# First expert layer: results weighed in the expert's own loop, the router's weights sent along in the slots, and the gather turned into transfers that add

## The chip, the cores and the metric

The kernel runs on one core of one Trainium2 chip. The metric is the device time of one launch in microseconds (us): the median of three runs. A profiled execution gives the trace: every instruction of the engines TensorE (PE), VectorE (DVE), ScalarE (ACT), GpSimd (POOL), of the queue of SyncE (SP), and every DMA, with times counted from the start of the span.

## What is computed

Four layers on x of 4 sequences of 512 tokens of width 256: a cross attention with 8 heads over a context of 1601 rows, a mixture of experts (E = 8, two experts for each token, a fixed capacity), a second cross attention, and a second mixture of experts. The change is in the first mixture of experts. Cut to what matters, the reference does this:

```python
x = x + attention(ctx, layernorm(x))
xf = layernorm(x).reshape(-1, 256)                       # 2048 tokens
scores = softmax(xf @ w_router)                          # 8 columns
expert_weights, top_experts = top_k(scores, 2)
# every (token, choice) gets a place in its expert's list, first come first served;
# beyond capacity = 512 places it is dropped
xb = zeros(8 * 512, 256).at[slot].set(xf[src])
y  = gelu(xb @ w1[e]) @ w2[e]                            # per expert
out[src] += expert_weights * y[slot]                     # dropped choices add 0
x = x + out + bias
# then the second attention and the second mixture of experts
```

## The kernel before

The kernel is one program that is fully laid out in advance. It has four stages, seen in the trace by the lines that run in them.

Stage A, 0 to about 1550 us: the first attention. Batch after batch, `route(b)` is slipped in between: it normalizes x[b] into `xn` (L159), computes the router's scores `sc`, takes the two best (values to `prob`, slot numbers to `slot`), and `send` (L316) scatters the token rows into `slot_x`, a tensor in device memory with 4096 rows (SLOTS) of 256 floats. One scatter moves 128 rows; there are 4 tiles of 128 tokens (t) and 2 choices (k) for each of the 4 batches, so 32 of them. The slots are set to zero early on by 8 transfers (`clear_slots`, L193) from a zeroed piece `empty` of the tile `scrap`.

Stage B, about 1550 to 1916 us: the experts. Each expert's list is worked through in two halves of 256 slots (`all_experts(0, ...)`, then `all_experts(1, ...)`). For each: `fetched` loads `sx` from `slot_x` (L1247) and the two weight matrices, `turned` transposes, `hidden` does the first product and the gelu on ACT (L1276), `results` does the second product, copies it out of PSUM (L1291), and stores it to `slot_y` (L1292). Between the halves there is a branch that repeats the experts if the halves were not filled as hoped; it is a meeting point for all engines. Right behind it stands `collect(0)`: for t, for k, POOL sets a buffer `g` to zero (L334) and gathers 128 rows of `slot_y` into it (L335). `add_collected(0)` (L352) multiplies each gathered tile by its `prob` column and adds it to x[0]. Then `queries(0)` starts the second attention's work on x[0]: moments of each tile (L127, L128), `ve` (L137), the square root `rs` on ACT (L144), the scaling (L159). `all_experts(1)` runs at the same time.

Stage C, about 1916 to 2560 us: the second attention, in 16 units of 13 steps. The order of the instructions on PE, DVE, ACT and POOL is written out by hand here: a table `at` holds what is to be issued in which step (`put`). For batch b, `collect(b + 1)` puts one gather in each of the steps max(52b - 28, 0) + 1 onwards (8 steps), `add_collected(b + 1)` puts two adds each in the steps 52b + 10, 12, 14 and 16, and `queries(b + 1)` begins at 52b + 12. From step 4 on, one step after the other, `clear_rows` sets 41 pieces of `rows_a` and `rows_b` (the second expert layer's lists) to zero by transfers on SP (L395) out of the small tile `empty`. Every second of these is preceded by a POOL memset that writes a marker into `empty` again (L1647); so the POOL memset waits for the two transfers that still read `empty`, and the next two transfers wait for the memset. `load_queries(u)` (L1160) brings the queries of unit u into `asked` on the same SP queue, at step 13u - 12. The maxima `tops` (L1195) and the running sums (L1471) are DVE's main work.

Stage D, about 2560 us to the end: the second mixture of experts. Its results are added onto the output in device memory by indirect transfers with an add (`add_out`, L1788).

Outside the stretches whose order is written out, the order of the instructions of each engine is chosen at compile time by a planner, from its own idea of durations. `keep_in_program_order` pins some transfers.

## Time and profile before

| | |
|---|---|
| median of 3 runs | 2829.24 us (2828.84 to 2831.44) |
| the profiled execution's own time | 2828.22 us |
| its span in the trace | 2826.2 us |
| PE busy | 2706.3 us of the span |
| DVE busy | 1468.9 us |
| ACT busy | 940.0 us |
| POOL busy | 260.0 us |
| PE busy in 1750 to 1930 us | 169.27 of 180 us |
| L335, gather without an add | 32 times, 1003 ns of POOL each (median) |
| L334, memset of `g` | 32 times, 314 ns of POOL each |
| L352, weigh and add | 32 times, 484 ns of DVE each |
| L1788, scatter with an add | 38 times, 1594 ns of POOL each |

Busy time is the sum of an engine's instructions. A line of the waits says which engine stood before which line, and what released it. A line of the timeline has the start, the duration, engine and line, and in brackets how long the engine had been idle before it and what ended that. Transfers issued by POOL are on the DMA queue q0, those of SP on q1.

### The profile page before, as it was taken

How to read it: one execution, taken by the hardware profiler on the slowest of the kernel's cores; microseconds unless marked ns; L12 is line 12 of the kernel's file. 1: busy time of each engine (PE TensorE's matmuls, PEld its weight loads, DVE VectorE, ACT ScalarE, POOL GpSimd, SP SyncE). 2: the span in 40 equal slices, each digit the busy share in tenths (PEclk: the TensorE clock that was granted, in tenths of full speed). 3: DMA queues.
4: the chain of work that ended last, by engine and by line, in shares of the span. 5: the costliest groups of instructions: out<-in, count | busy, mean ns of one | idle time of the engine just before them, and what ended most of it. 6: DMA issues, size and time to landing. Idle time of an engine off the chain costs nothing. (4 is left out here: it accounts for less than half of the span.)

```text
span 2826.2 us, 36019 instructions
## 1 busy us (share of the span) xinstructions
PE 2706.3 (96%) x13566; PEld 1851.0 (65%) x13566; DVE 1468.9 (52%) x2343; ACT 940.0 (33%) x1362; POOL 260.0 (9%) x292
## 2 busy tenths in 40 slices
PE   5999999999999999999999899998999898889998
PEld 2666666666766666766666687774455454458887
DVE  6544547544476444545444421137887878872111
ACT  3333334323233332333233211214444444442221
POOL 0000000100000000001000002001110201022542
PEclk9999999999999999999999999999999999999999
DMA  5444443433343344334334545535631111025573
GB/s 164 110 115 113 104 103 95 114 95 84 95 119 91 102 100 100 89 85 113 95 84 125 176 154 175 169 97 144 178 81 40 38 31 54 33 71 193 166 229 89
DMA packets 196435, 311.95 MB, mean 110 GB/s; under 512 B 43319, under 2 KB 117368, under 8 KB 193560
## 3 DMA queue, kind: packets, MB, share of 16 engines
q1 hardware_dynamic: 157512, 227.52, 29.4%
q0 software_dynamic: 14160, 46.31, 5.5%
q10 hardware_dynamic: 24576, 35.68, 4.9%
q8 instruction: 111, 1.82, 0.3%
q14 instruction: 76, 0.62, 0.1%
HBM read 111.73 MB, written 51.34 MB: 58 GB/s over the span
## 5 line engine op out<-in xcount | busy, mean ns | idle before, releaser
L842 DVE TENSOR_REDUCE top<-ps_s 128x1 f32<-128x2113 f32 x128 | 301.8, 2358 | 581.0 <-PE ps_s L834 581.0
L871 PE MATMUL ps_o<-pT,v 128*128 128x256 f32 x2176 | 521.6, 381 | 0.5 <-DVE inv L849 0.5
L834 PE MATMUL ps_s<-kT,qT 128*128 128x512 f32 (+1 forms) x1280 | 489.0, 526 | 5.8 <-ACT attn L848 5.8
L871 PEld LDWEIGHTS ps_o<-pT,v 128*128 128x128 f32 x2176 | 409.9, 191 | 115.1 <-issue 68.4
L848 ACT ACTIVATE attn<-ps_s,top 128x2113 f32<-128x2113 f32 x128 | 259.0, 2024 | 476.7 <-DVE top L842 452.0
L834 PEld LDWEIGHTS ps_s<-kT,qT 128*128 128x128 f32 x1280 | 241.6, 191 | 252.5 <-issue 236.6
L863 DVE STREAM_TRANSPOSE pT<-swapped 128x2176 f32<-128x2176 f32 x128 | 312.4, 2441 | 33.8 <-DMA swapped<-attn 23.7
L1195 DVE TENSOR_REDUCE tops<-ps_s 128x2 f32<-128x1024 f32 (+1 forms) x224 | 238.3, 1106 | 102.9 <-PE ps_s L1184 101.7
L783 PE MATMUL ps_k<-kvin,wkv 128*128 128x512 f32 (+1 forms) x640 | 263.6, 535 | 4.1 <-DVE mv_g L721 2.1
L1453 PE MATMUL ps_w<-asked,keyed 64*128 64x256 f32 (+1 forms) x1664 | 225.2, 405 | 35.1 <-DVE tops L1195 33.9
L817 PE MATMUL ps_v<-wkv,kvin 128*128 128x256 f32 x1088 | 254.5, 381 | 0.0
L1466 ACT ACTIVATE pT<-ps_w 128x1024 f32<-128x1024 f32 x192 | 189.8, 1022 | 150.7 <-PE ps_w L1453 139.4
L817 PEld LDWEIGHTS ps_v<-wkv,kvin 128*128 128x128 f32 x1088 | 204.8, 190 | 34.9 <-issue 4.5
L1453 PEld LDWEIGHTS ps_w<-asked,keyed 64*128 64x128 f32 (+1 forms) x1664 | 150.3, 188 | 110.2 <-DVE tops L1195 53.5
L1471 DVE TENSOR_TENSOR sum<-sum,pT 128x1024 f32<-128x1024 f32 x176 | 214.8, 1221 | 13.5 <-PE ps_o L1480 4.9
L796 ACT ACTIVATE kT<-ps_k,bqk 128x512 f32<-128x512 f32 (+1 forms) x160 | 96.9, 620 | 265.9 <-PE ps_k L783 130.5
L783 PEld LDWEIGHTS ps_k<-kvin,wkv 128*128 128x128 f32 x640 | 116.2, 192 | 78.6 <-issue 68.0
L824 ACT COPY v<-ps_v 128x512 f32<-128x512 f32 x144 | 79.9, 561 | 215.9 <-PE ps_v L817 143.9
L1184 PE MATMUL ps_s<-kv,qT 32*128 32x512 f32 (+1 forms) x1024 | 134.7, 553 | 9.3 <-DVE tops L1195 5.1
L1269 PE MATMUL ps_h<-sxT,w 128*128 128x256 f32 x512 | 116.1, 384 | 3.7 <-ACT hT L1276 3.7
L1283 PE MATMUL ps_y<-w,hT 128*128 128x256 f32 x512 | 115.1, 380 | 0.0
L1269 PEld LDWEIGHTS ps_h<-sxT,w 128*128 128x128 f32 x512 | 97.9, 192 | 20.5 <-ACT hT L1276 4.5
(302 smaller groups left out, 2525.2 us busy)
## 6 DMA issues: line engine op xcount, KB each, us to landing
swapped<-attn SPq DMA_DIRECT2D x1536, 68.0 KB, 2.0
swapped<-attn ACTq DMA_DIRECT2D x512, 68.0 KB, 2.2
w<-in_w_dram SPq DMA_DIRECT2D x32, 1024.0 KB, 6.0
rows_b<-empty SPq DMA_DIRECT2D x36, 530.0 KB, 4.4
w_e<-in_wall_dram SPq DMA_DIRECT2D x5, 2052.0 KB
cw<-in_ctxT_dram SPq DMA_DIRECT2D x4, 1601.0 KB
keyed<-kv SPq DMA_DIRECT2D x32, 200.1 KB, 3.6
ctx_b<-in_ctx_dram SPq DMA_DIRECT2D x3, 1536.0 KB
```

Of the source, the lines that this page charges most:

```text
L783: nc.tensor.matmul(ps[:, :n], lhsT=wkv[:, c, hs], rhs=kvin[:, c, : NB - 1, k, :] if k < 4 else kvin[:, c, NB - 1, :, :], start=c == 0, sto ...
L817: nc.tensor.matmul(ps[:, k, :], lhsT=flat_kvin[c][:, j * P : (j + 1) * P], rhs=wkv[:, c, cols], start=c == 0, stop=c == DC - 1,)
L834: nc.tensor.matmul(flat[:, j0 : j0 + n], lhsT=qT[:, t * P : (t + 1) * P], rhs=kT[:, j0 : j0 + n], start=True, stop=True,)
L842: nc.vector.tensor_reduce(top, flat[:, :L], AX.X, ALU.max, negate=True)
L848: nc.scalar.activation(attn[:, :L], flat[:, :L], AF.Exp, bias=top, accum_out=total)
L863: nc.vector.transpose(pT[:, :, k * P : (k + 1) * P].rearrange("p c (a i) -> p a c i", a=4), swapped.rearrange("p a (c i) -> p a c i", i=32),)
L871: nc.tensor.matmul(ps, lhsT=v[:, j - parts[part][0], (h % 2) * DH0 : (h % 2 + 1) * DH0], rhs=pT[:, j, :], start=j == 0, stop=j == NB - 1,)
L1195: nc.vector.tensor_reduce(tops[u][:, t : t + at // n, 2 * pair : 2 * pair + 2, j0 // 512], of, AX.X, ALU.max,)
L1269: nc.tensor.matmul(ps[:, f, :], lhsT=w1[:, c, (f0 + f) * P : (f0 + f + 1) * P], rhs=sxT[:, c, :], start=c == 0, stop=c == DC - 1,)
L1453: nc.tensor.matmul(ps[:r, s, pair * QH : (pair + 1) * QH], lhsT=keyed[o][64 * s : 64 * s + 64, pair, j * P : j * P + r], rhs=asked[u % 3][ ...
L1466: nc.scalar.activation(pT[:r], ps[:r], AF.Exp)
L1471: nc.vector.tensor_tensor(sums[u, 0], sums[u, 0], pT, ALU.add)
```

## The change

The rows in the slots become 264 floats wide (XROW): behind the 256 values of a token stand its 8 router scores. They are copied there before the choice is made, sent along by the same scatter and fetched with `sx`. The expert's own column of them, `share`, is copied out in `turned`, and `results` multiplies by it when it empties PSUM; an unused slot holds zeros. `slot_y` so holds weighed results. `collect` has no buffer, no memset and no add on DVE any more: the gather itself adds onto x[b], tile by tile, and its order is now k outside and t inside. `add_collected` and `prob` are gone, with their steps in the table of stage C and their place in `keys_next`.

```diff
-    slot_x = dram.tile([SLOTS, D], F32, name="slot_x")
+    slot_x = dram.tile([SLOTS, XROW], F32, name="slot_x")            # XROW = D + E
...
-                zeros.unsqueeze(1).to_broadcast([P, 4, D]),
+                zeros.unsqueeze(1).to_broadcast([P, 4, XROW]),
...
-        xn = wide_rt.tile([P, NT, D], F32, tag="xn", name="xn")
+        xw = wide_rt.tile([P, NT, XROW], F32, tag="xn", name="xw")
+        xn = xw[:, :, :D]
...
+            nc.vector.tensor_copy(xw[:, :, D:], sc)
             for k in range(2):
-                pk, ck, hk, cand = prob[k][:, mine_b], small(f"c{k}"), wide(f"hot{k}"), wide("cand")
+                pk, ck, hk, cand = small("pk"), small(f"c{k}"), wide(f"hot{k}"), wide("cand")
...
-                        in_=xn[:, t, :],
+                        in_=xw[:, t, :],
...
         def one_of(t, k):
             j = b * NT + t
-            g = gat.tile([P, D], F32, tag="g", name="g")
-            nc.gpsimd.memset(g, 0.0)
             nc.gpsimd.indirect_dma_start(
-                out=g,
+                out=x[b][:, t, :],
                 out_offset=None,
                 in_=slot_y[:, :],
                 in_offset=bass.IndirectOffsetOnAxis(ap=slot[k][:, j : j + 1], axis=0),
                 bounds_check=SLOTS - 1,
                 oob_is_err=False,
+                compute_op=ALU.add,
             )
-            got.append(g)
-
-        return got, [lambda t=t, k=k: one_of(t, k) for t in range(NT) for k in range(2)]
-
-    def add_collected(b, got, tiles=range(NT)):
-        for t in tiles:
-            for k in range(2):
-                j = b * NT + t
-                xs = x[b][:, t, :]
-                nc.vector.scalar_tensor_tensor(
-                    xs, got[2 * t + k], prob[k][:, j : j + 1], xs, ALU.mult, ALU.add
-                )
+        return [lambda t=t, k=k: one_of(t, k) for k in range(2) for t in range(NT)]
...
-        empty = scrap[:, 0, :]
+        empty = scrap.rearrange("p t d -> p (t d)")[:, :XROW]
...
-            sx = two.tile([P, CT, D], F32, tag="sx", name="sx")
+            sx = two.tile([P, CT, XROW], F32, tag="sx", name="sx")
...
+            share = two.tile([P, CT], F32, tag="share", name="share", bufs=3)
+            nc.vector.tensor_copy(share, sx[:, :, D + e])
...
-            nc.vector.tensor_copy(y, ps)
+            nc.vector.tensor_tensor(y, ps, share.unsqueeze(2).to_broadcast([P, CT, D]), ALU.mult)
             nc.sync.dma_start(slots(slot_y, e, half), y)
...
-                if k == 6:
-                    add_collected(0, got0)
...
-                for k, f in enumerate(steps):
+                for k, f in enumerate(collect(b + 1)):
                     put(max(s0 - 28, 0) + 1 + k, f)
-                for t in range(NT):
-                    put(
-                        s0 + 10 + 2 * t,
-                        lambda b=b, got=got, t=t: add_collected(b + 1, got, (t,)),
-                    )
```

`share` is handed on from `turned` through `hidden` to `results`; the tile that `output_bias` borrows from `scrap` moves from its second row to its third.

More of the change, by code (lines that the diff above doesn't have):

```diff
@@ L43 @@
 SLOTS = E * CAP
+XROW = D + E
 HALF = CAP // 2
@@ L224, in xattn_ffn_twice @@
     reached = const.tile([P, 2, E], F32, name="reached")
-    prob = [const.tile([P, NX], F32, name=f"prob{k}") for k in range(2)]
     slot = [const.tile([P, NX], I32, name=f"slot{k}") for k in range(2)]
@@ L327, in collect @@
     def collect(b):
-        got = []
         def one_of(t, k):
             j = b * NT + t
-            g = gat.tile([P, D], F32, tag="g", name="g")
-            nc.gpsimd.memset(g, 0.0)
             nc.gpsimd.indirect_dma_start(
-                out=g,
+                out=x[b][:, t, :],
                 out_offset=None,
@@ L896, in output_bias @@
         def output_bias():
-            values_bias = scrap[:, 1, :P]
+            values_bias = scrap[:, 2, :P]
             ps = ps_t.tile([P, D], F32, tag="t", name="ps_bo")
@@ L1260, in turned, with hidden @@
             nc.vector.tensor_copy(sxT, tp.rearrange("p c t q -> p c (t q)"))
-            return e, half, sxT, w1, w2
-        def hidden(e, half, sxT, w1, w2):
+            share = two.tile([P, CT], F32, tag="share", name="share", bufs=3)
+            nc.vector.tensor_copy(share, sx[:, :, D + e])
+            return e, half, sxT, share, w1, w2
+        def hidden(e, half, sxT, share, w1, w2):
             hT = two.tile([P, FC, HALF], F32, tag="hT", name="hT")
@@ L1276, in hidden, with results @@
                 nc.scalar.activation(hT[:, f0 : f0 + 2, :], ps, AF.Gelu_apprx_tanh)
-            return e, half, hT, w2
-        def results(e, half, hT, w2):
+            return e, half, hT, share, w2
+        def results(e, half, hT, share, w2):
             ps = ps_y.tile([P, CT, D], F32, tag="y", name="ps_y")
@@ L1358, in xattn_ffn_twice @@
                     results(*hidden(*turned(*fetched(e, half))))
-        got0, steps = collect(0)
-        for f in steps:
+        for f in collect(0):
             f()
@@ L1612, in xattn_ffn_twice @@
                 put(s0 + 1, lambda b=b: begin(b + 1))
-                got, steps = collect(b + 1)
-                for k, f in enumerate(steps):
+                for k, f in enumerate(collect(b + 1)):
                     put(max(s0 - 28, 0) + 1 + k, f)
-                for t in range(NT):
-                    put(
-                        s0 + 10 + 2 * t,
-                        lambda b=b, got=got, t=t: add_collected(b + 1, got, (t,)),
-                    )
                 def later(b=b):
```

## Prediction

> **What bounds the kernel now.** I read the page first, then the windows by stage, then what PE waits for, then the timelines around each place where the change acts.

> ```profile
> PE 2706.3 (96%) x13566; PEld 1851.0 (65%) x13566; DVE 1468.9 (52%) x2343; ACT 940.0 (33%) x1362; POOL 260.0 (9%) x292
> ...
> 1750.00:1930.00 180.00, 169.27 (x819) 129.82 (x819) 50.41 (x75) 35.56 (x56) 16.03 (x21) 0.96 0.45 144
> 1950.00:1975.00 25.00, 20.85 (x210) 10.71 (x206) 21.63 (x30) 9.92 (x12) 0.29 (x3) 0.93 0.66 179
> 2090.00:2115.00 25.00, 25.00 (x226) 14.90 (x223) 22.87 (x34) 13.31 (x18) 9.04 (x14) 1.00 0.09 25
> 2260.00:2285.00 25.00, 25.00 (x224) 15.56 (x218) 22.91 (x32) 11.87 (x15) 0.00 (x0) 1.00 0.20 48
> ```

> PE is the bound (second column of the windows: PE busy, fourth: DVE). A gain or loss is a gain or loss of PE's idle time. The last three windows hold the adds of batches 1, 2 and 3 that the change takes away: only the first has idle PE time.

> Where does PE wait near the change? In stage B, behind the branch, and in stage C, at three adds and at the start of unit 4:

> ```profile
> 1769.04 0.20 ACT L144 ACTIVATE rs<-ve 128x4 f32<-128x4 f32 x1 [3.97 <-DVE ve L137]
> 1771.20 3.78 PE L1269 MATMUL ps_h<-sxT,w 128*128 128x256 f32 x8 [3.38 <-ACT hT L1276]
> ...
> 1954.39 1.13 PE L1453 MATMUL ps_w<-asked,keyed 64*128 64x256 f32 x8 [1.38 <-DVE tops L1195]
> 1960.57 1.39 PE L1453 MATMUL ps_w<-asked,keyed 64*128 64x256 f32 x8 [2.33 <-DVE tops L1195]
> 2056.71 2.09 PE L1453 MATMUL ps_w<-asked,keyed 64*128 64x256 f32 x16 [1.18 <-DMA asked<-qT]
> ```

> The first pair: ACT sits at the square root for x[0] until the gathers of x[0] have landed and been added, the gelu behind it is late, and PE loses 3.38 us. The last line is a transfer of queries. It was late because on SP's queue it stands behind the zeroing of `rows_b`, and that runs in lockstep with POOL:

> ```profile
> SPq L395 <- POOL empty L1647: 62.5, 13, 6.1
> POOL empty L1647 <- DMA rows_b<-empty: 102.2, 16, 9.5
> ```

> (waits from 1916 to 2060 us). Memset, two transfers, memset: about 7 us a round, from 1924.07 until beyond 2056. So the start of unit 4 is set by POOL, SP and the DMA engines, not by PE or DVE, and PE is there 1.18 us early.

> **The change part by part.**

> *DVE's 32 adds go* (484 ns each, 15.5 us). Eight in stage B: DVE is busy 50 of 180 us there. Eight at 1952 to 1971: each pair takes 1.00 us and PE waits right behind three of them (1.38, 2.33, and 0.44 at 1972.48). At most 0.92 + 1.00 + 0.44 = 2.4 us come back. But all of it lies ahead of unit 4, which waits for `asked`: PE only gets there earlier and waits longer. Worth 0; if the zeroing did not bind, 2.4 + 1.18 = 3.6. Sixteen at 2096 to 2114 and 2264 to 2282: PE is busy 25.00 of 25.00, worth 0.

> *POOL's 32 memsets go* (314 ns), and the gathers become adding transfers. No gather of before adds, but `add_out` does:

> ```profile
> L335 POOL DMA_INDIRECT g<-slot_y,slot x32: 994/1003/1653, 1750.0 to 2115.8; - x32
> L1788 POOL DMA_INDIRECT out_dram<-y,to x38: 1549/1594/1621, 2559.5 to 2816.0; - x38
> ```

> (nanoseconds: least, median, most). Bounds for an issue are 1.00 and 1.59 us; I take 1.59, since it is the only row that adds. The gap between issues is 0.30 us where nothing is waited for. On the DMA engines:

> ```profile
> q0 software_dynamic: 384, 1.04, 13.6%
> rows_b<-empty SPq DMA_DIRECT2D x8, 530.0 KB, 4.7
> g<-slot_y,slot POOLq DMA_INDIRECT x8, 5.4
> ...
> q0 software_dynamic: 437, 0.32, 18.0%
> out_dram<-y,to POOLq DMA_INDIRECT x4, 3.8
> ```

> The first is the window 1998 to 2028 us (eight gathers beside the zeroing): 13.6% of 30 us for 1.04 MB, 3.9 us of all 16 engines per MB. The second is 2800 to 2816 us (adds alone): 18.0% of 16 us for 0.32 MB, 9.0 us per MB, 2.3 times as much. [...]

> *What that does to the zeroing.* In program order four gathers of batch 1 stand ahead of the first memset of `empty` (steps 1 to 4). Before: 1918.26 to 1924.07. After: 4 x 1.59 + 3 x 0.30 = 7.26 us, so 1925.5: +1.45 (with 1.00 us an issue it would be -0.9). Then twelve gathers run inside the chain: four of batch 1 and eight of batch 2. The four rounds with two gathers of batch 2 took 7.38, 7.54, 7.50 and 7.48 us; the rounds without 7.08 in the mean. [...] Bounds 0 and +3.1; the upper one is taken, as it stands on the row. Sum: `asked` of unit 4 comes 4.5 us later, and PE with it. Behind it, unit 5's queries were issued at 2071.3 for use near 2091, so nothing more is late.

> *The waits that are added.* A k = 1 gather changes the same tile as the k = 0 gather four issues earlier and must wait for its landing. The scatters into `slot_x` show such a wait: POOL stood 71.8 us in 28 of them. Transfers to separate parts of one tile do not wait (the four of `keyed` on SP went out within 3.22 us), so I expect the four tiles of x[b] to stay independent. In stage C: four issues later is 7.6 us, landings took 5.4, and behind a waiting gather stands the memset of `empty`, which waits for its transfers anyway (4.57 and 3.45 us): 0. For batch 2 the gathers are four rounds apart in pairs: 0. Batch 3's come behind the zeroing, the old wait of POOL for DVE there (25.9 us) goes, and x[3] is needed from 2264 on: 0.

> *collect(0) in stage B.* The eight gathers went out at 1750.0 to 1759.2, one every 1.3 us; the weights of the next experts filled the DMA engines (landings 7.0 us), the last landed at about 1766.8. After: issues at 1750.0, 1751.9, 1753.8, 1755.7; the next four each wait for their first half. With 7.7 us to land under load (the four adds at 2556 to 2600 us), the fourth is in at 1763.4, the eighth goes out then and lands at 1771.1: 4.3 us later. Behind it there was one add, two moments and `ve`, 2.0 us; now one moment and `ve`, 0.8. So ACT's root comes 3 us later, and PE's 3.38 us become about 6.4: **+3.0**, if the planner leaves the root in front of the gelus. Bounds: it may move the root behind them (-3.4), or in front of more, or the landings may take the 9.2 us of the slowest add (+4.5).

> *Small parts.* `y` becomes a multiplication from PSUM with 512 columns: L573 does that in 681 ns, the copy took 692: 0. `share`, 16 copies of about 0.17 us, and four copies of `sc` (L474, 128x32, 0.18 us): DVE waits for PE in both stages (581 us at L842, 99.8 at L1291): 0; without that cover 3.4 us. Rows of 1056 bytes: scatters of 1060-byte rows land in 3.2 us (`rows_b`) and 2.6 (`rows_a`) against 2.8, so -0.2 to +0.4 each, in chains that end 30 us ahead of the load of the second half. The zeroing of `slot_x` moves 3% more, hidden by the 250 us to the first scatter. [...]

> **Sum.** +4.5 (unit 4) + 3.0 (root) = +7.5 us. The sum is made on the profiled execution (span 2826.2, its own time 2828.22); the median is 1.0 above it, and I add the sum to the median: 2829.24 + 7.5 = 2836.7.

> **The rivals.**

> 1. *Both lags* (above), 2836.7. For: both waits are in the trace already, at their edge. Own range +3 to +13 (2832 to 2842).
> 2. *One lag or none.* The planner orders stage B anew, and with the adds gone it may put the root behind the gelus (-3.4), or SP's transfer of `asked` one round earlier (7 us), so that unit 4 no longer waits and the 3.6 us of stage C count. One lag alone gives +3 to +4.5; the rest -3.4 + 4.5 = +1. So 2825 to 2833.
> 3. *Faster: POOL sends gathers at 1.00 us and the zeroing gets ahead.* Price: -0.9 at the start instead of +1.45. It decides once `asked` is in place before PE is: then 3.6 in stage C and 3.4 in stage B, -7.0, 2822. Against it: the only adding row says 1.59.
> 4. *Each adding gather waits for the one before it*, or `asked` slips by a round. With landings of 5 us in place of a step of 1.9: three waits ahead of the first memset, 3 x 3.1 = 9, and about 4 us in each later round with gathers: +12 to +40, 2841 to 2870. Against it: the `keyed` row.

> **How the numbers follow.** 0.2% of this time is 5.7 us, about what a measurement can tell from no change. Chances: case 1 0.52 (0.37 slower, 0.15 within), case 2 0.25 (0.20 within, 0.03 faster, 0.02 slower), case 3 0.08 (0.07 faster, 0.01 within), case 4 0.15 (slower). Together slower 0.54, within 0.36, faster 0.10. The range 2825 to 2848 takes in case 1 and nearly all of case 2, and the near third of case 4; 0.17 lies outside.

> **What would show it.** Right: L1788-like issues of 1.5 to 1.6 us for the gathers; the first memset of `empty` about 7.3 us after the first gather of batch 1; PE's wait for `asked` at unit 4 grown from 1.18 to some 8 us, with the three waits near 1952 to 1972 smaller; a wait of 6 us for L1276 behind L144 in stage B; windows of batches 2 and 3 unchanged. Wrong: no wait for `asked`, or gathers that go out one by one at their landings.

## The result, and the profile after

The changed kernel is slower: 2842.01 us against 2828.97 us (medians of 6 runs each on one chip), ratio 1.0051 with a 95% interval of 1.0041 to 1.0061, so +13 us where +7.5 was forecast. It lies in the stated range of 2825 to 2848 us, at the upper end of what was said for the likeliest case (2832 to 2842). On two other chips the same pair gave 1.0031 (1.0021 to 1.0040) and 1.0037 (1.0021 to 1.0052). The profiled execution after took 2845.54 us, span 2843.8, at the slow end of its runs; its span is 17.6 us above that of before.

The page's line of engines, and the same stretches as before (columns: the window, its length, then PE, PEld, DVE, ACT and POOL busy, PE's granted clock, DMA share, GB/s). Stage C begins some 3 to 4 us later than before, so the last three windows are moved by 4 us:

```profile
PE 2716.0 (96%) x13566; PEld 1854.9 (65%) x13566; DVE 1457.7 (51%) x2331; ACT 939.7 (33%) x1362; POOL 271.2 (10%) x260
...
1750.00:1930.00 180.00, 165.74 (x783) 128.32 (x783) 45.15 (x72) 33.60 (x54) 19.26 (x14) 0.95 0.46 137
1954.00:1979.00 25.00, 22.61 (x238) 11.79 (x230) 22.38 (x27) 11.64 (x14) 0.39 (x4) 1.00 0.54 144
2094.00:2119.00 25.00, 25.00 (x197) 14.33 (x193) 20.44 (x25) 14.40 (x20) 0.27 (x1) 1.00 0.05 9
2264.00:2289.00 25.00, 25.00 (x204) 14.37 (x206) 20.60 (x26) 14.70 (x21) 0.00 (x0) 1.00 0.03 7
```

Stage B lost 3.5 us of PE's busy time (169.27 to 165.74). At the adds of batch 1 PE is busier, at those of batches 2 and 3 it was full and is full. DVE has 11 us less to do, POOL 11 us more, although its 32 memsets are gone.

What PE and ACT waited for in stage B, and PE in stage C. In a timeline the brackets hold the idle time before the line and what ended it:

```profile
1759.31 1.28 ACT L145 ACT_TABLE_LOAD   x1
1771.92 0.20 ACT L145 ACTIVATE rs<-ve 128x4 f32<-128x4 f32 x1 [11.33 <-DVE ve L138]
1772.15 1.28 ACT L1269 ACT_TABLE_LOAD   x1
...
1774.09 5.76 PE L1262 MATMUL ps_h<-sxT,w 128*128 128x256 f32 x16 [6.56 <-ACT hT L1269]
...
1961.02 1.14 PE L1443 MATMUL ps_w<-asked,keyed 64*128 64x256 f32 x8 [0.46 <-DVE tops L1186]
...
1966.28 1.13 PE L1443 MATMUL ps_w<-asked,keyed 64*128 64x256 f32 x8 [1.42 <-DVE tops L1186]
...
1970.85 2.00 PE L1443 MATMUL ps_w<-asked,keyed 64*128 64x256 f32 x16
...
2063.32 3.89 PE L1443 MATMUL ps_w<-asked,keyed 64*128 64x256 f32 x16 [4.58 <-DMA asked<-qT]
```

The root `rs` of x[0] stands in front of the gelus as before, ACT has loaded the root's table at 1759.31 and then waits 11.33 us for `ve`, and PE's wait behind it has grown from 3.38 to 6.56 us. In stage C the three waits at the adds fell from 1.38, 2.33 and 0.44 us to 0.46, 1.42 and nothing. In stage B the wait for `sx` at L1250 grew too, from 0.23 to 1.72 us, just ahead of the one for `hT`. The wait for `asked` at unit 4 grew from 1.18 to 4.58 us, and the 16 matmuls behind it took 3.89 us instead of 2.09.

POOL's gathers in stage B and around the start of the zeroing:

```profile
1749.48 1.63 POOL L335 DMA_INDIRECT x<-slot_y,slot  x1 [28.12 <-DVEq L1348]
...
1756.99 1.55 POOL L335 DMA_INDIRECT x<-slot_y,slot  x1 [0.30 <-issue]
1759.81 1.55 POOL L335 DMA_INDIRECT x<-slot_y,slot  x1 [1.26 <-DMA x<-slot_y,slot]
...
1763.53 1.55 POOL L335 DMA_INDIRECT x<-slot_y,slot  x1 [0.30 <-issue]
...
1921.63 1.55 POOL L335 DMA_INDIRECT x<-slot_y,slot  x1 [156.54 <-DMA slot_y<-y]
1928.22 0.65 POOL L1631 MEMSET empty<- 128x1 f32 x1
```

and the groups of waits of SP's queue and of POOL from 1916 to 2060 us (engine, line, waited for: us in total, times, longest):

```profile
SPq L386 <- POOL empty L1631: 103.4, 18, 9.8
...
POOL empty L1631 <- DMA rows_b<-empty: 92.3, 15, 10.4
...
POOL x L335 <- issue: 6.2, 15, 0.7
```

A gather now holds POOL for 1.55 us instead of 1.00. The lines at 1756.99 and 1759.81 us are the fifth and the sixth gather of x[0]. The fifth waits for nothing; the sixth waits 1.26 us for a landing, by the order that of the second, which changes the same tile. That is the only wait of a gather for another one: in stage C the list has none. SP and POOL run in lockstep as before.

The DMA engines in 2004 to 2034 us, where the eight gathers of batch 2 run beside the zeroing (queue: packets, MB, share of 16 engines; then issues with us to landing):

```profile
q0 software_dynamic: 1076, 0.98, 25.2%
...
x<-slot_y,slot POOLq DMA_INDIRECT x8, 5.7
```

25.2% of 30 us for 0.98 MB is 7.7 us of all engines per MB, against 3.9 before: in these two windows an adding gather costs twice what a plain one does, in 1076 packets instead of 384.

**Where the time went.** The same matmul of PE, looked up in both traces from the start of each span, is early or late in the trace after as follows: ahead of the branch -0.5 us, behind `collect(0)` +3.4, at 2040 us +3.2, behind unit 4's start +9.0, at 2300 us +10.4, at 2530 us +15.1, at the end +17.6. The two steps of +3.9 and +5.8 lie at the two waits of the forecast. What is behind 2100 us goes with stretches of half clock that are not at one place: the granted clock fell to 0.5 for 37.5 us of stage C in the trace before, 64.9 in this one, and 41 to 61 in single traces of the kernels below. That part does not follow the change. From 2100 to 2810 us this trace loses 5.8 us on that of before; two kernels below that gather plainly (`plain_all`, `fac_before_asked`) lose 6.6 and 6.3, and the changed kernel taken again (`after_again`) gains 2.9.

### The profile page after: what moved, and what is told of

Same layout as the page of the kernel before. It is cut to its first block, busy times and chain, and to the rows that moved or that the text cites. A ratio compares the mean times of both kernels' runs of the same rounds, so it can differ in the third digit from the quotient of the medians.

```text
span 2843.8 us, 35938 instructions
## 1 busy us (share of the span) xinstructions
PE 2716.0 (96%) x13566; PEld 1854.9 (65%) x13566; DVE 1457.7 (51%) x2331; ACT 939.7 (33%) x1362; POOL 271.2 (10%) x260
## 5 line engine op out<-in xcount | busy, mean ns | idle before, releaser
L1443 PE MATMUL ps_w<-asked,keyed 64*128 64x256 f32 (+1 forms) x1664 | 232.7, 416 | 35.2 <-DVE tops L1186 30.5
L1276 PE MATMUL ps_y<-w,hT 128*128 128x256 f32 x512 | 115.1, 380 | 0.0
```

What stands on the lines that cost most here:

```text
L1443: nc.tensor.matmul(ps[:r, s, pair * QH : (pair + 1) * QH], lhsT=keyed[o][64 * s : 64 * s + 64, pair, j * P : j * P + r], rhs=asked[u % 3][ ...
```

## The experiments

The first four kernels ran on one chip, with before at 2830.55 us (67 runs).

**Is it the adding gathers at all?** In `plain_all` all four batches are gathered as before, with a zeroed buffer and an add on DVE (without the weight, which `results` has applied); wide rows, `share` and the multiplication stay. `plain0` does so for x[0] alone.

```diff
-                out=x[b][:, t, :],
+                out=to,                      # a zeroed tile of gat
...
-                compute_op=ALU.add,
...
+            nc.vector.tensor_tensor(xs, got[t, k], xs, ALU.add)
```

> The weights still travel in the slots and the experts weigh their own results, but all four batches are gathered as before: a zeroed buffer, a plain gather, an add on DVE (now a plain add of two tiles). Theory of the two lags (the adding gathers delay the root of x[0] in stage B and the queries of unit 4 in stage C): both waits go back to those of before, so 2829 us, +-3. Rival 'wide rows' (the 264-float rows, the share copies and the multiplication out of PSUM cost the time): it stays at 2842.

> Only batch 0 is gathered plainly and added on DVE; batches 1 to 3 keep the adding gathers. Two lags: stage B gets its 3 to 4 us back (PE's wait behind the root 3.4 instead of 6.6 us), stage C keeps its lag, so about 2838. Rival 'stage C alone': no change, 2842. Rival 'stage B alone, the rest follows from it': 2829.

`plain_all`: 2830.40 us (14 runs), ratio 1.0007 (0.9998 to 1.0016). `plain0`: 2833.54 us (22 runs), 1.0012 (1.0003 to 1.0020). PE's waits from 1740 to 2600 us that stand at the two places, first of `plain_all`, then of `plain0`:

```profile
PE ps_h L1276 <- ACT hT L1283: 3.2, 1, 3.2
PE ps_w L1460 <- DMA asked<-qT: 0.6, 1, 0.6
```

```profile
PE ps_w L1460 <- DMA asked<-qT: 6.9, 1, 6.9
PE ps_h L1276 <- ACT hT L1283: 2.8, 1, 2.8
```

With plain gathers both waits are about as before (3.4 and 1.2 us), and so is the time: the rows of 1056 bytes, `share` and the multiplication cost nothing that a measurement can tell; the interval leaves room for 4.5 us. With plain gathers for x[0] alone, only the first wait goes back; the second stays long. So each wait belongs to its own gathers: the one in stage B to those of x[0], the one at unit 4 to those of batches 1 to 3. For `plain0` 2838 us were expected and 2833.54 came; the changed kernel itself did not run on this chip, so what `plain0` gained on it there is not known.

How long a wait is does not say what it costs. Unit 4 in `plain_all` and in `plain0`:

```profile
2056.23 2.10 PE L1460 MATMUL ps_w<-asked,keyed 64*128 64x256 f32 x16 [0.61 <-DMA asked<-qT]
```

```profile
2057.37 3.86 PE L1460 MATMUL ps_w<-asked,keyed 64*128 64x256 f32 x16 [6.91 <-DMA asked<-qT]
```

The wait is 6.3 us longer, but unit 4 starts only 1.1 us later: PE was there 5.2 us sooner (2050.46 instead of 2055.62), most of it the 4 us that it gains where the adds of batch 1 are gone. To the 1.1 us come some 2.5 us behind the wait, where the 16 matmuls take 3.86 us instead of 2.10, as they take 3.89 in the trace after at a granted clock of 0.50. Together that is 3.6 us; the medians of the two kernels differ by 3.1.

**Is it the two waits?** `after_root` keeps the adding gathers, but binds the root of x[0] on ACT to program order, so that it no longer stands in front of the gelus. `after_asked` issues the transfer of queries for units 4, 8 and 12 seven steps earlier; in its trace that of unit 4 went out at 2035.96 instead of 2058.71.

```diff
+        if b == 0:
+            with in_order(nc.scalar):
+                root = ln_root(turns, mv, NT, ve)
...
-            put(NM * u - 12, lambda u=u: load_queries(u))
+            put(NM * u - (19 if u % 4 == 0 else 12), lambda u=u: load_queries(u))
```

> The changed kernel with the square root for x[0] pinned behind the gelu that stands ahead of it in the source, so that it no longer stands in front of the gelus of the first experts of the second half. Two lags: PE's 6.6 us behind the root vanish, 2842 - 6.6 = 2835.5, or a little less as PE also stays warm. Rival 'DVE is the one that is late' (the moments of x[0] wait on DVE in front of the transposed rows that PE needs): the wait moves to another line and the time stays within 2 us of 2842.

> The changed kernel with the queries of the units 4, 8 and 12 put on SP's queue seven steps earlier, ahead of the late rounds of the zeroing. Two lags: PE's 4.6 us at unit 4 vanish together with the time at half clock behind it (about 2 us), and stage B's lag stays: about 2835. Rival 'the zeroing's lockstep only shifts, something else binds unit 4' : PE waits for another thing there and the time stays at 2842.

`after_root`: 2832.52 us (21 runs), 1.0012 (1.0006 to 1.0019). `after_asked`: 2831.99 us (21 runs), 1.0006 (0.9999 to 1.0014). The same list of waits, `after_root` first:

```profile
PE ps_w L1447 <- DMA asked<-qT: 7.7, 1, 7.7
```

```profile
PE ps_h L1262 <- ACT hT L1269: 5.5, 1, 5.5
```

Each edit takes away its own wait and leaves the other. But each also left a time within 2 us of before, some 3 us below what was expected, as if either wait alone were the whole loss. The root's edit mends something that before had as well (its 3.4 us), so a comparison with before can't divide the loss. The next two sets were made for that.

**A clock that stays up, and both edits.** The second set ran on a chip on which before took 2840.04 us (25 runs). `after_again` is the changed kernel once more. `after_warm` puts useless products in front of unit 4, so that PE is not idle there. `after_both` has both edits of above, `before_both` has them in the kernel before.

```diff
+        def warm():
+            ps = side.tile([P, 2, D], F32, tag="m", name="ps_warm")
+            for _ in range(8):
+                nc.tensor.matmul(ps, lhsT=ident, rhs=wT[:, 2], start=True, stop=True)
+        put(4 * NM - 1, warm)
```

> The changed kernel itself once more, so that its time stands beside the others in one call with as many runs. Both theories: 2842, that is 1.004 to 1.005 of before. If the two lags are all there is, it lies above each of the one-sided repairs by the repair.

> The changed kernel with eight products of no use (128x512, about 0.5 us each) put on PE at the end of the step before unit 4, where PE otherwise waits 4.6 us for the queries. They take nothing from the wait's end, they only keep PE busy in it. Theory 'a wait of PE costs twice, by itself and by the half clock that follows': the matmuls behind it run at full speed (2.0 instead of 3.9 us for the first sixteen), and the time falls by 2 to 4 us to about 2838 or 2839. Rival 'the half clock is independent of this wait': no gain, or a loss of up to 4 us.

> The changed kernel with both repairs, the pinned root and the early queries. Two lags, adding up: 2842 - 6.6 - 6.6 = 2829; if the repairs overlap (each alone already gave most of it): 2828 to 2832. Rival 'something third in the change costs time': it stays 3 us or more above the kernel before with the same two repairs.

> The kernel before with the same two repairs. It has 3.4 us of wait behind the root and 1.2 us at unit 4 to win, with some half clock behind them: 2830.5 - 4.6 = 2826, down to 2823. This is what the changed kernel with both repairs must be held against: two lags says that the two then lie within 3 us of each other, the changed one lower by up to 2.4 us for the eight adds of DVE in stage C.

| kernel | median, us | ratio to before (95%) |
|---|---|---|
| `after_again` | 2849.18 (6 runs) | 1.0037 (1.0021 to 1.0052) |
| `after_warm` | 2847.82 (18 runs) | 1.0026 (1.0018 to 1.0033) |
| `after_both` | 2826.16 (5 runs) | 0.9949 (0.9936 to 0.9961) |
| `before_both` | 2823.51 (6 runs) | 0.9939 (0.9927 to 0.9951) |

PE's timeline at unit 4, `after_again` first, then `after_warm`:

```profile
2068.93 3.87 PE L1443 MATMUL ps_w<-asked,keyed 64*128 64x256 f32 x16 [14.78 <-DMA asked<-qT]
```

```profile
2051.01 7.13 PE L1637 MATMUL ps_warm<-cw,ident 128*128 128x512 f32 x16
2064.87 3.86 PE L1443 MATMUL ps_w<-asked,keyed 64*128 64x256 f32 x16 [6.73 <-DMA asked<-qT]
```

`after_warm` says nothing on the clock: on this chip the wait was 14.8 us long, the products filled 7.1 us of it, 6.7 us of idle time were left, and the matmuls behind took as long as without them (3.86 and 3.87 us). A gain of 2 to 4 us was expected; the medians differ by 1.4, and the intervals of the two ratios overlap. It would have told something only where the products cover the whole wait.

The two kernels with both edits beat both kernels, and PE's list of waits has neither wait in them. Between them there is no difference that five and six runs can tell: the medians are 2.7 us apart, and the difference is known to some 5 us. So without the two waits no loss is left that these runs show. On this chip the two edits took 16.5 us from before, where 4.6 to 7.5 were expected; before was not profiled on it, so where the rest came from is not shown. PE in 1760 to 1800 us, first of after, then of `after_both`:

```profile
1760.00:1800.00 40.00, 31.72 (x130) 24.29 (x129) 9.39 (x27) 8.98 (x16) 4.48 (x3) 0.91 0.55 166
```

```profile
1760.00:1800.00 40.00, 39.40 (x176) 31.68 (x175) 8.06 (x20) 8.31 (x15) 2.98 (x2) 1.00 0.68 217
```

PE is busy 39.4 of 40 us instead of 31.7, with 176 matmuls instead of 130, at full clock. Before had 36.6 of 40 us here. The two traces are of different chips.

**How much is each wait's?** The third set ran on one more chip, before at 2832.39 us (59 runs). Its four kernels are the changed kernel (`fac_none`), the same with the root's edit (`fac_root`), the same with the edit of the queries (`fac_asked`), and before with the edit of the queries (`fac_before_asked`).

> The changed kernel, beside its one-sided repairs in one call and on one chip, since the time at unit 4 depends on the chip: its rounds of the zeroing took 7.0 us in the first trace and 7.4 in another, and PE's wait for the queries 4.6 and 14.8 us. Two lags: 1.004 to 1.005 of before.

> The changed kernel with the pinned root alone. PE's 6 us behind the root go, and as the last results of stage B and with them the zeroing come earlier by the same amount, unit 4 moves too: two lags says 5 to 7 us below fac_none. Rival 'unit 4 takes it all back' (its start does not move): 0 to 1 us below fac_none.

> The changed kernel with the early queries alone. Two lags: PE's wait at unit 4 goes, 4.6 us on a chip with rounds of 7.0 us, up to 14.8 on one with 7.4, and some 2 us of half clock behind it; so 6 to 15 us below fac_none. The rival 'stage B is what costs' says at most 2 us below fac_none.

> The kernel before with the early queries alone. On a chip with rounds of 7.0 us it waited 1.2 us there, on one with 7.4 us the queries come some 7 us later: so 1 to 8 us below before. If the changed kernel's loss sits in unit 4, the difference between fac_none and before shrinks by what fac_asked wins more than this one does, to the 3 to 4 us of stage B.

| kernel | median, us | ratio to before (95%) | left in PE's waits |
|---|---|---|---|
| `fac_none` | 2841.21 (22 runs) | 1.0031 (1.0021 to 1.0040) | `asked` 5.8, `hT` 5.6 us |
| `fac_root` | 2833.16 (22 runs) | 1.0004 (0.9995 to 1.0013) | `asked` 7.3 us |
| `fac_asked` | 2834.31 (14 runs) | 1.0010 (1.0000 to 1.0020) | `hT` 6.7 us |
| `fac_before_asked` | 2831.05 (14 runs) | 0.9992 (0.9984 to 1.0000) | `hT` 3.8 us |

The edit of the queries takes 2841.21 - 2834.31 = 6.9 us from after and 2832.39 - 2831.05 = 1.3 us from before. So the change's part at unit 4 is 6.9 - 1.3 = 5.6 us. With that edit in both, what is left of the change is 2834.31 - 2831.05 = 3.3 us: stage B's part, less what PE gains at the adds of batch 1 and, with the queries early, no longer waits away. The two add up to the 8.8 us between `fac_none` and before, by the way they are worked out; what they tell is the division. Each ratio's interval is 2 to 3 us to either side, so each part is known to some 4 us only; that both are there is also what the waits of the traces say.

The division hangs on the order. The root's edit alone takes 2841.21 - 2833.16 = 8.1 us from after (5 to 7 were expected), nearly all of the loss, although `asked` is then still waited for (7.3 us). Before with the root's edit alone was not run, so the part of unit 4 with the root mended in both stays open.

## Why the prediction was right, and which terms were off

The likeliest case, both lags, is what happened: slower, by the two waits that the trace of before had at their edge; two edits of order take both away, and the loss with them. The places and the direction were right by their reasons. That the sum came near is in part luck: one of its terms has nothing behind it, and one that was missing made up for it. Point by point:

- *The issue of an adding gather*: 1.55 us measured, 1.59 taken. The nearest row was the right one, and the rival that stood on 1.00 us fell with it.
- *collect(0)*: +3.0 forecast; `rs` came at 1771.92 instead of 1769.04, +2.9, and PE behind it +3.9 in the pair of traces; in the other five traces of the changed kernel with this root and adding gathers for x[0], the same stretch (1740 to 1780 us) costs 4.0 to 4.7 us more than in that of before, in the two with plain gathers and the old root (`plain_all`, `fac_before_asked`) 0.0 and 0.1. The eighth gather went out at 1763.53, where 1763.4 was forecast, but not for the reason given: seven steps of 1.86 us and one wait of 1.26 us (of the sixth) brought it there, not the landing of the fourth. The bound of +4.5 for landings of 9.2 us was mis-summed: two landings stand in that chain, so 1.5 us more for each makes +6.0.
- *The three adds at 1952 to 1972*: the waits shrank by 0.92, 0.91 and 0.44 us, 2.3 together, of at most 2.4. PE gained more than that: from 1945 to 1975 us the trace after gains 4.1 us on before, and so does every trace with adding gathers for batch 1, on all the chips, while the three further ones with plain gathers gain 0.0 to 0.3. The rest is clock: before has a stretch of half clock at 1961.3 us, after has none between 1948.9 and 2061.6. It brought nothing, as the step said, and for the reason given: unit 4 waits for `asked`, and PE only waits longer. That PE was still 3.2 us late at 2040 us has another cause: from 1916 to 1945 it had lost 4.2 us. One place of that loss, in PE's timeline of before and then of after:

```profile
1918.14 2.00 PE L1453 MATMUL ps_w<-asked,keyed 64*128 64x256 f32 x16 [2.54 <-DVE tops L1195]
```

```profile
1921.52 3.68 PE L1443 MATMUL ps_w<-asked,keyed 64*128 64x256 f32 x16 [2.54 <-DVE tops L1186]
```

  The idle time ahead is the same, 2.54 us; the matmuls took 1.7 us longer, as the granted clock was 0.50 there (1921.6 to 1925.0 us). This loss does not come from the change: the three further traces with plain gathers have 2.4 to 4.2 us of it. The trace of before is the only one of fourteen without any; the others have at least 0.9 us.
- *The zeroing, +4.5 forecast*: +3.6 in this pair of traces, but only +0.8 of it for a reason that was given. `asked` went out at 2058.71 instead of 2051.74, 7.0 us later, of which 3.4 came from stage B with the first gather of batch 1 (1921.63 instead of 1918.26). The first memset started 6.59 us behind that gather instead of 5.81: +0.8, not +1.45; the other traces of adding gathers show the same. The first seven rounds behind it took 55.90 us instead of 53.12, +2.8. But the four late gathers of batch 1 are in the first two of the seven (+0.7); the five behind them, with no gather in them, have the other +2.1. The ten rounds after these, with all of batch 2, took 72.07 and 72.04 us. And where kernels with plain and with adding gathers ran on one chip, the first seven rounds do not tell them apart: 55.2 us with plain (`plain_all`) against 53.7 to 54.4 with adding ones, 53.9 (`fac_before_asked`) against 54.6 to 54.8, 58.0 (`before_both`) against 56.5 to 56.7. So no run shows the term of +3.1. It was the author's estimate, +0.26 us for each of twelve gathers: in the trace of before a gather cost its round 0.2 us (7.38 to 7.54 us with two, 7.08 without), and times the 2.3 of `add_out`'s row that is 0.46. Each gather did take twice the engines' time, but the rounds did not follow it; what the +2.8 of this pair comes from is not shown, and that it lies near +3.1 is luck. With plain gathers, too, the seven rounds took from 53.1 to 58.0 us in the four traces.
- *The price on the DMA engines*: 2.0 times a plain gather (7.7 us of all engines per MB against 3.9), where the row of `add_out` gave 2.3.
- *Unit 4*: the step of PE is +5.8 us in the pair of traces, 5.6 by the last four kernels, +4.5 forecast. The term that was missing is the clock. PE's windows around the wait, before and then after (the granted clock is the third figure from the end):

```profile
2055.50:2059.00 3.50, 2.32 (x28) 1.90 (x28) 3.50 (x4) 1.02 (x2) 0.10 (x1) 1.00 0.42 137
2059.00:2063.00 4.00, 3.75 (x40) 1.92 (x32) 3.63 (x4) 2.26 (x4) 0.00 (x0) 1.00 0.72 164
```

```profile
2058.00:2063.30 5.30, 0.74 (x8) 0.01 (x1) 5.20 (x5) 0.00 (x0) 0.10 (x1) 0.84 0.90 236
2063.30:2067.00 3.70, 3.68 (x16) 3.19 (x16) 0.55 (x1) 1.02 (x1) 0.00 (x0) 0.50 0.77 226
2067.00:2072.00 5.00, 4.75 (x42) 2.28 (x40) 2.09 (x2) 2.41 (x3) 0.10 (x1) 0.86 0.35 80
```

```profile
1913.50:1916.90 3.40, 2.10 (x13) 0.88 (x11) 1.96 (x3) 0.00 (x0) 0.00 (x0) 1.00 0.21 72
1916.90:1920.30 3.40, 2.16 (x18) 1.86 (x20) 1.09 (x1) 0.95 (x1) 1.76 (x3) 1.00 0.08 19
```

```profile
1918.20:1921.60 3.40, 0.86 (x10) 0.11 (x3) 2.80 (x3) 0.00 (x0) 0.00 (x0) 1.00 0.23 77
1921.60:1925.00 3.40, 3.40 (x16) 2.80 (x16) 0.00 (x0) 1.37 (x2) 3.07 (x2) 0.50 0.28 38
```

  In before the idle time falls into two windows, each with PE busy for over 2 us, and the clock stays up; in after it lies in one, with 0.86 us of work left, and the next window is at half clock. Here a wait of 4.6 us or more is to be sized with what comes behind it, 2.0 to 2.6 us.
- *Small parts, 0*: `plain_all` shows it, to within 0.0016 of the time. The longer wait for `sx` in stage B, 1.3 to 3.1 us in all six traces of the changed kernel with this root, is not the wide rows': with them and plain gathers for x[0] it is not there. It stands just ahead of the wait for `hT`, so it adds nothing.

The other rivals: no gather waited for its neighbour in stage C, and the root was not moved. The forecast's sum of 7.5 us stands against 8.8 us on the chip of the third set, where the two parts make all of it by the way they are worked out, and against 13 us on the first. The pair of traces there has some 8 us behind 2100 us, in half clock that other traces have with plain gathers too; whether the six runs of the changed kernel fell so by chance stays open.

## What to carry to other kernels

An add that is moved from an engine with time to spare into a transfer is not free (here POOL's issue took 1.55 us instead of 1.00, and the transfer 2.0 times the DMA engines' time): ask what stands behind the issue on that queue. Look in the trace for waits of one to three microseconds that are there already: a change that delays what ends them pays there, and waits that grew to 4.6 us and more were paid again here in the clock, with 2.0 to 2.6 us. A wait that grows because the engine comes sooner is no loss by itself: compare when the work behind it starts. Put a repair into the old kernel too before you count it for the new one: here two edits of order were worth more in the old kernel (0.9939) than the change cost. And one pair of traces can have luck in it: a difference that a third trace without the change shows too is not the change's.

## What the runs showed of the hardware

The changed kernel waited for the same transfer 4.6, 5.8 and 14.8 us in its traces on three chips. From the fourth on, the rounds of the zeroing took 6.6 to 7.8 us in the first of these traces and 7.3 to 8.2 us in the one with 14.8 us; there `asked` went out 5.1 us later (2063.76) and PE was there 4.6 us sooner (2054.15 against 2058.74). So a transfer that comes a little late on one chip can be far too late on another. In the windows of batch 2 a gather that adds had packets of about 0.9 KB where a plain one had 2.7 (0.98 MB in 1076, 1.04 in 384), took 2.0 times the engines' time, and landed little later (5.7 us against 5.4).
